# A transformer block with cross-attention on one core: the sums of proj_w are made beside the second group's attention instead of the first's

## The chip, the cores and the metric

The kernel runs on one core of a Trainium2 chip. The metric is the time in device microseconds (us) of one execution, and before stands at a median of 676.46 us. A core has a matrix engine, TensorE (PE; its weight loads are shown as PEld), three engines for work on elements, VectorE (DVE), ScalarE (ACT) and GpSimd (POOL), and the queue SP (SyncE) from which all transfers of this kernel are issued. TensorE multiplies one stationary tile with one moving tile and adds into a bank of PSUM; the other engines move results into SBUF.

## The reference

Eight sequences of 256 tokens with 512 channels (x) attend to eight contexts of 256 tokens (ctx_2048). The inputs are float32, and so are all products.

```python
x = layer_norm(hidden_states, ln1_w, ln1_b)
q = (x @ q_w + q_b).reshape(B, LQ, H, HD).transpose(0, 2, 1, 3)
k = (encoder_hidden_states @ k_w + k_b).reshape(B, LK, H, HD).transpose(0, 2, 1, 3)
v = (encoder_hidden_states @ v_w + v_b).reshape(B, LK, H, HD).transpose(0, 2, 1, 3)
scores = jnp.einsum('bhqd,bhkd->bhqk', q, k) * scale
scores = jnp.where(mask, scores, mask_value)
attn = jax.nn.softmax(scores, axis=-1)
out = jnp.einsum('bhqk,bhkd->bhqd', attn, v)
out = out.transpose(0, 2, 1, 3).reshape(B, LQ, D)
hidden = out @ cproj_w + cproj_b + residual
y = layer_norm(hidden, ln2_w, ln2_b)
y = jax.nn.gelu(y @ fc_w + fc_b, approximate=True)
return hidden + (y @ proj_w + proj_b)
```

There are 16 heads of 32 channels. fc_w is 512 x 2048 and proj_w is 2048 x 512.

## The kernel before, in words

**Groups and stages.** The eight sequences are two groups of four (g is 0 or 1). Per group: layer norm, the products q, k and v, the attention, the output product o, a second layer norm (norm_y, turn_y), the first product of the MLP (fc, with fc_w), gelu, and the second one (pd, with proj_w). Stages of the two groups overlap: while TensorE makes group 0's attention it also makes group 1's k, v and q, and while it makes group 1's attention it also makes group 0's o and fc.

**Strassen products.** Each large product is made by Strassen's scheme in Winograd's form: seven products of half-size blocks (P1 to P7) in place of eight, which needs sums of blocks of both operands ahead of the products. `quad` (line 837) makes the seven products with their evictions (t1, t2, t3, c11, c12, c21, c22: VectorE or ScalarE copies or adds a bank of PSUM to SBUF). The two MLP products use two levels, 49 small products; `grown2` (line 1212) and `grown` (line 1146) walk the outer seven in the order 1, 6, 2, 5, 3, 7, 4. So fc016_P5 is group 0, half 1 of the hidden columns, outer product 6, inner product 5.

**Sums of the MLP weights.** `mlp_weight_sums` (line 1062) makes them for a weight's half s (0 or 1): four quarters are loaded, four outer sums of 1024 columns (pw0s1 to pw0s4 for half 0 of proj_w), then for each of the seven outer operands four inner sums of 256 columns (pw0i6_1 and so on). Every sum may run on VectorE or on GpSimd. The results are stored to DRAM (prd0_6_False for an outer sum, prd0_6_True for the inner ones) and are read back piece by piece when the product pd needs them (loads pl). For proj_w that is 32 loads of 128 KB, 8 outer and 56 inner sums, and 22 stores; `proj_sums` (line 1094) issues them. fc_w has the same with fw, fcd and fl, and has no part in the change.

**One unit of attention.** A unit is one group, one set of four heads and one sequence: unit 121 is group 1, the third set of heads (8 to 11), sequence 1. `scores` (line 991) issues for it: the score product s121 (TensorE); eight evictions ev121 (ScalarE); two row maxima mx121 (VectorE, transposing as they reduce), a transpose mt and a fold of them on VectorE with three copies mc on ScalarE between; a store md and a load mm that spread the maximum over all partitions; two subtractions less121 (VectorE, or GpSimd in two pieces of 512 columns); two exponentials exp121 (ScalarE). `attend` (line 1039) then issues the attention product av121 (TensorE), its inverse of the row sums r121 (three instructions on VectorE) and the scaling att121. A group has 16 units (`units_of`); the written streams put av three units behind s.

**The order.** Nothing is decided at run time. The text `PROGRAM` (lines 124 to 353) names all 2927 steps in one fixed order, and a letter after a colon says which engine does a step that has a choice: V is VectorE, A is ScalarE, G is GpSimd; without a letter it is the step's first alternative. `Order.run` (line 94) goes through the words and issues the steps in that order, so each engine and the queue SP work through their own steps strictly in it:

```python
for word in PROGRAM.split():
    name, _, e = word.partition(":")
    o = ops.pop(name)
    o.eng = letters[e] if e else o.alts[0][0]
```

The text `PLACES` (lines 355 to 468) gives each buffer its slot of SBUF or its bank of PSUM in the same way; a slot is used by many buffers one after the other, and a step waits until the slot's earlier buffer has been read for the last time. Step names in the profile are buffers' names: pr holds a unit's scores and exponentials, mx its maxima, mm the spread maximum, rc and r the inverse, pw0s and pw0i sums of proj_w, h the result of fc, z1t and z1i sums of it ahead of pd, ps_y the transposes after the second layer norm.

**Where the sums of proj_w stand in before.** Between s000 and s100, the first score products of the two groups, the text has 60 of the 64 sums (24 on VectorE, 36 on GpSimd), 31 of the 32 loads and 19 of the 22 stores; the rest follow later. The lines of `PROGRAM` with s003 to av003 are 186 to 196, those with s121 to av121 are 232 to 244.

Of the kernel before, what the change touches and what calls it, by code (L numbers as in the profile page):

```python
# [148 lines left out]
ct1_3 mx000_1 fw1i7_1:G q0_0_P4 fw0i4_3:G q0_1_P7 q0_0_c21 aggr_x1_10 q0_1_c11 k0_0_c21 q0_1_P5 aggr_x1_11
fw0i3_2:V mt000 fw0i3_4:V mc000_2 fw1i6_1:V mc000_3 fcd0_3_True mc000_1 fw1i3_2:V s020 q0_1_t3:A fw1i6_2:V fold000  # L150
fw1i3_4:G q0_1_c22 q0_0_P3 md000 fw1i6_3:G ev020_01 ev020_30 fcd1_3_True eps_x1_1 ev020_10 pow_x1_1 ct1_7 ev020_31
ev020_21 fw1i7_2:G q0_1_P4 ev020_20 q0_0_c12:V fw0i4_1:G ev020_00 mx020_1 ev020_11 fw1i7_4:G s002 fw1i6_4:V
fcd1_7_True q0_1_c21 ct1_6 v0_0_P7 mx020_0 ct1_5 ev002_30 ev002_11 ct1_2 ev002_31 nb_x1_1 mt020 mm000 ev002_00
fw0i4_2:V ev002_10 fcd1_6_True v0_1_P7 mc020_3 v0_0_c22 mc020_2 pw0_00_01 ev002_01 fw0i4_4:V ev002_21 mx002_0
mc020_1 ev002_20 s022 mx002_1 q0_1_P3 ev022_20 fold020 ev022_10 ev022_31 mt002 v0_1_c22 md020 ev022_30 less000_0:G
ev022_21 vd0_0_12 turn_c1_31 ev022_11 kd0_0_22 turn_c1_21 ev022_01 mc002_1 turn_c1_00 kd0_1_11 ev022_00 v0_0_P4
# [199 lines left out]
cq0_00=42 cq0_10=82 cq0_01=60 cq0_11=58 ps_cols=3 ps_c0_00=0 c0_00=64 ps_c0_10=4 ps_c0_20=4 c0_10=46 ps_c0_30=3  # L356
ps_c0_01=0 c0_01=62 ps_c0_11=4 ps_c0_21=1 c0_11=56 ps_c0_31=4 xt0_0=34 xt0_1=58 xt0_2=32 xt0_3=63 xt0_4=83 xt0_5=33
xt0_6=14 xt0_7=23 st_x0_0=9 mv_x0_0=8 rs_x0_0=2 xn_x0_00=65 xn_x0_01=22 st_x0_1=4 mv_x0_1=5 rs_x0_1=4 xn_x0_10=5
# [1111 lines left out]
```

## Time and profile before

| | us |
|---|---|
| three runs | 677.11, 676.02, 676.46 |
| median | 676.46 |
| the profiled execution, its own time | 676.35 |
| its span, first to last instruction | 674.6 |
| TensorE busy | 663.8 (4001 matmuls) |
| VectorE busy | 578.3 (969 instructions) |
| GpSimd busy | 379.1 (340 instructions) |
| ScalarE busy | 340.1 (699 instructions) |
| mean granted clock of TensorE | 0.997 of full speed |

A row of the profile that groups instructions names the code line, the engine, the operation, the output and the inputs by their buffers with partitions x elements, the count after x, then the busy time in us and the mean duration of one in ns, then the idle time of the engine just before them and what ended most of it. A row with a time in front is one instruction, or several that run back to back: start, duration, engine, line, and in square brackets how long the engine had been idle and for whom. A row of TensorE's waits gives the total in us, the count and the longest. All matmuls have one line (641), so they are told apart by the buffer names. Times in these rows are us from the start of the span.

### The profile page before, as it was taken

Reading aid. Unit: us, or ns where it says so; the run is one execution under the profiler, and the core shown is the slowest. Engines: PE = TensorE matmul, PEld = TensorE weight load, DVE = VectorE, ACT = ScalarE, POOL = GpSimd, SP = SyncE. Lnnn points to the kernel's source line nnn. Section 1 sums busy time; section 2 is a strip of 40 time slices with the busy share of each in tenths; the row PEclk is TensorE's granted clock in tenths of the full one; section 3 lists DMA queues with packets and bytes.
Section 4 is the critical chain, followed back from the end, with each engine's and each line's share of the span. In section 5 each row is a group of like instructions: output and inputs, shape, how many; then the busy total and the mean of one; then the engine's idle time right before and its main releaser. Section 6 shows DMA issues by size and latency. Waiting matters only on the chain.

```text
span 674.6 us, 11523 instructions
## 1 busy us (share of the span) xinstructions
PE 663.8 (98%) x4001; PEld 498.3 (74%) x4001; DVE 578.3 (86%) x969; ACT 340.1 (50%) x699; POOL 379.1 (56%) x340
## 2 busy tenths in 40 slices
PE   9999999999899999999999999999999999999997
PEld 7674564478544676777687888888888888888886
DVE  2889889999999999999889999998489877896874
ACT  1246488768999979976764872001040221930000
POOL 1552556575578999977945743310636247518542
PEclk9999999999989999999999999999999999999999
DMA  8989888987957635445552646997999586842686
GB/s 264 329 273 337 306 286 257 295 258 211 307 164 241 210 113 203 157 142 170 174 190 95 220 130 167 267 245 250 165 243 237 133 243 149 232 144 57 192 166 118
DMA packets 173034, 140.65 MB, mean 209 GB/s; under 512 B 83712, under 2 KB 133424, under 8 KB 172976
## 3 DMA queue, kind: packets, MB, share of 16 engines
q1 hardware_dynamic: 172976, 139.92, 70.5%
q8 instruction: 32, 0.52, 0.3%
q14 instruction: 26, 0.21, 0.1%
HBM read 102.00 MB, written 37.88 MB: 207 GB/s over the span
## 4 chain that ended last, share of the span: by engine, by line
PE 92%; DVE 4%; DMA 3%; ACT 1%; issue 0%; SPq 0%; POOL 0%; DVEq 0%
PE fc_X L641 14%; PE pd_X L641 14%; PE fc_W L641 7%; PE pd_W L641 7%; PE av L641 6%; PE s L641 4%; PE k_X L641 4%; PE v_X L641 4%; PE q_X L641 4%; PE o_X L641 4%; PE pd_Y L641 4%; PE fc_Y L641 3%; PE k_W L641 2%; PE v_W L641 2%; PE o_W L641 2%; PE q_W L641 2%
## 5 line engine op out<-in xcount | busy, mean ns | idle before, releaser
L621 ACT ACTIVATE pr<-s,cols 128x256 f32<-128x256 f32 x256 | 103.1, 480 | 30.5 <-PE s L641 24.5
L1029 POOL TENSOR_TENSOR pr<-pr,mm 128x512 f32<-128x512 f32 x74 | 98.1, 1353 | 28.8 <-ACT pr L621 9.5
L1004 DVE TRANSPOSE_TENSOR_REDUCE mx<-pr 128x32 f32<-128x1024 f32 x64 | 77.6, 1222 | 1.9 <-ACT pr L621 1.8
L1209 ACT ACTIVATE h<-h,cols 128x256 f32<-128x256 f32 x128 | 54.6, 496 | 48.4 <-DVE h L632 45.5
L1032 ACT ACTIVATE pr<-pr 128x1024 f32<-128x1024 f32 x64 | 66.9, 1066 | 3.8 <-POOL pr L1029 2.9
L632 DVE TENSOR_TENSOR h<-fc_X,h 128x512 f32<-128x512 f32 x80 | 53.0, 678 | 10.0 <-PE fc_X L641 8.3
L641 PE MATMUL av<-pr,ones 128*32 128x256 f32 x512 | 35.1, 392 | 3.5 <-ACT pr L621 3.3
L632 DVE TENSOR_TENSOR h<-fc_W,h 128x512 f32<-128x512 f32 x48 | 32.1, 680 | 5.1 <-PE fc_W L641 4.9
L1024 DVE TENSOR_TENSOR pr<-pr,mm 128x1024 f32<-128x1024 f32 x27 | 34.8, 1310 | 0.9 <-DMA mm<-md 0.9
L1011 ACT COPY mx<-mx 32x64 f32<-32x64 f32 x96 | 23.3, 243 | 16.6 <-DVE mx L1008 13.4
L630 POOL TENSOR_TENSOR z1i<-z1t,z1i 128x512 f32<-128x512 f32 x12 | 16.8, 1420 | 26.0 <-issue 16.3
L641 PEld LDWEIGHTS av<-pr,ones 128*32 128x32 f32 x512 | 14.4, 110 | 21.8 <-issue 5.9
L632 POOL TENSOR_TENSOR h<-h,fl 128x512 f32<-128x512 f32 x16 | 21.4, 1350 | 8.6 <-DVE h L632 7.5
L613 ACT ACTIVATE e<-pd_X,cols 128x256 f32<-128x256 f32 x4 | 1.9, 468 | 44.1 <-PE pd_X L641 31.9
L641 PE MATMUL fc_W<-y1i,fl 128*128 128x256 f32 x92 | 22.8, 379 | 0.0
L641 PE MATMUL pd_X<-z1i,pl 128*128 128x256 f32 x96 | 22.0, 379 | 0.0
L796 POOL TENSOR_TENSOR rs_y<-rs_y,neg_half 128x2 f32<-128x2 f32 x8 | 8.2, 1034 | 23.4 <-DVE rs_y L793 22.8
L1012 DVE TENSOR_REDUCE mx<-mx 32x32 f32<-32x256 f32 x32 | 18.5, 580 | 2.4 <-ACT mx L1011 2.2
L641 PE MATMUL pd_W<-z1i,pl 128*128 128x256 f32 x88 | 20.5, 379 | 0.0
L641 PEld LDWEIGHTS pd_X<-z1i,pl 128*128 128x128 f32 x96 | 18.2, 190 | 2.5
L641 PEld LDWEIGHTS fc_W<-y1i,fl 128*128 128x128 f32 x92 | 17.5, 190 | 2.4
L641 PE MATMUL pd_X<-z0i,pl 128*128 128x256 f32 x80 | 19.0, 380 | 0.0
(593 smaller groups left out, 1836.3 us busy)
## 6 DMA issues: line engine op xcount, KB each, us to landing
mm<-md SPq DMA_DIRECT2D x32, 512.0 KB, 4.9
pl<-prd SPq DMA_DIRECT2D x52, 256.0 KB, 4.4
fl<-fcd SPq DMA_DIRECT2D x41, 256.0 KB, 4.1
fl<-prd SPq DMA_DIRECT2D x18, 256.0 KB, 4.6
fw<-in_L_xattn_fc_w_dram SPq DMA_DIRECT2D x16, 256.0 KB, 5.3
pw<-in_L_xattn_proj_w_dram SPq DMA_DIRECT2D x32, 128.0 KB, 3.1
hid<-in_x_dram SPq DMA_DIRECT2D x8, 512.0 KB, 3.6
hd<-hid SPq DMA_DIRECT2D x8, 512.0 KB
```

Of the source, the lines that this page charges most:

```text
L621: lambda e: nc.scalar.activation(to(), of_(), AF.Identity, bias=bias(), scale=1.0))
L630: nc.gpsimd.tensor_tensor(to()[:, ts(k, 512)], in0()[:, ts(k, 512)], in1()[:, ts(k, 512)], op)
L632: E[e].tensor_tensor(to(), in0(), in1(), op)
L641: nc.tensor.matmul(o(), l(), r(), start=first, stop=True, skip_group_check=True)
L796: lambda e, rs=rs: nc.gpsimd.tensor_tensor(tile_of(rs)[:, 2:4], tile_of(rs)[:, 0:2], neg_half[:, 0:2], ALU.pow), lock=True)
L1004: T.op(f"mx{u}_{h}", [("DVE", 1.126)], [(pr[h], None)], [(mx, [h])], lambda e, h=h: nc.vector.tensor_reduce(tile_of(mx)[:, 0:64].rearrange ...
L1011: lambda e, a=a: nc.scalar.copy(tile_of(mx)[0:32, 64 + 64 * a : 128 + 64 * a], tile_of(mx)[32 * a : 32 * a + 32, 64:128]))
L1012: T.op(f"fold{u}", [("DVE", 0.38)], [(mx, [2, 3, 4, 5])], [(mx, [6])], lambda e: nc.vector.tensor_reduce(tile_of(mx)[0:32, 320:352], tile_ ...
L1024: nc.vector.tensor_tensor(p_, p_, m_[:, :, None, :].to_broadcast([P, 2, 2, S]), ALU.subtract)
L1029: E[e].tensor_tensor(p_, p_, at(M, j)[:, None, :].to_broadcast([P, 2, S]), ALU.subtract)
L1032: lambda e, h=h: nc.scalar.activation(tile_of(pr[h]), tile_of(pr[h]), AF.Exp), table="exp")
L1209: lambda e, f=f, b=b, c=c: nc.scalar.activation(at(h[f][b], c), at(h[f][b], c), AF.Gelu_apprx_tanh, bias=col(c_fcb + f * 4 + c), scale=1.0 ...
```

## The change

The changed kernel differs only in the two texts `PROGRAM` and `PLACES`. It has the same 2927 steps, so the same products, sums, loads and stores, in another order, and 234 of them stand on another engine: VectorE gets 981 instructions in place of 969, ScalarE six fewer, GpSimd 11 fewer. The queue SP has the same 565 transfers in another order. 1040 of 1301 buffers have another slot.

The sums of proj_w move. In the first group's attention (s000 to s100) one sum and four loads are left. Three sums, ten loads and one store stand between s100 and the first transpose of the second layer norm (turn_y0_00). Between that and the last attention product (av133) stand 55 sums, 18 on VectorE (12 inner, 6 outer) and 37 on GpSimd, with 18 loads and 19 stores; five sums and two stores follow later. In the same stretch VectorE makes 8 halves of the subtractions less and GpSimd 11, where before it was 3 and 17.

All other steps keep their dependencies, but their order was written anew along the whole program, so the neighbours of nearly every step differ. Of the text the two stretches are shown that hold s003 to av003 and s121 to av121, before (-) and after (+), and the first line of the places.

```diff
 PROGRAM = """
...
-prd0_4_True v1_1_P3 less032_0:V norm_x1_20:A fold021 s003 v1_0_c22 md021 av001 pw1i4_4:V ev003_30 v1_0_c12:V
-pw1i1_3:G ev003_10 ev003_01 pw1i1_1:V ev003_31 pw1i1_2:V ev003_21 v1_1_P7 pw1i1_4:G ev003_11 pw1_01_10 exp032_1
-pw1s1:V pw1_01_00 pw1_01_01 ev003_20 ev003_00 pw1_01_11 r001 turn_x1_31 pw1s2:G exp032_0 prd1_4_True turn_x1_21
-turn_x1_11 mm021 mx003_1 x1_31:A av032 prd1_1_True v1_1_c12:A mx003_0 x1_21:A pw1i2_3:G mt003 q1_0_P1 pw1i2_1:G
-att001 mc003_3 v1_1_c22 x1_11:A pw1i2_2:G r032 mc003_2 mc003_1 pw1i2_4:G ab0_000 s023 fold003 pw1s3:V md003 v1_1_P4
-ev023_20 ku033 ev023_31 pw1i6_3:V ev023_21 prd1_7_False less021_0:V ev023_11 ev023_10 turn_x1_01 ev023_30 pw1i6_1:V
-v1_0_P4 ev023_00 mm003 less021_1:V ev023_01 prd1_6_False x1_01:A ow10 att032 exp021_1 pw1s4:G s011 vd0_1_21
-v1_0_c21 ku013 mx023_1 exp021_0 vd0_1_12 q1_1_P1 prd1_5_False ev011_30 mx023_0 ev011_00 pw1i6_2:G ev011_20 ev011_11
-av021 mt023 ev011_21 pw1i6_4:V ev011_10 x1t1:V prd1_6_True ev011_01 fl012_2 ev011_31 q1_0_t1:A less003_0:V s031
-mc023_1 mc023_2 mc023_3 pw1i7_1:V less003_1:V ev031_01 exp003_0 fold023 pw1i7_2:G exp003_1 mx011_0 md023 pw1i5_1:G
-ev031_21 vu013 x1t2:G ev031_20 r021 ev031_30 prd1_2_True av003 ev031_10 ev031_00 att021 ev031_31 mx011_1 ev031_11
...
+x1_20:V md001 v1_0_P5 x1_30:A less032_0:V x1_00:A nb_x1_2 v1_0_c11 s003 mm001 pw0_00_10 mt021 v1_0_t3:V v1_1_P2
+norm_x1_21:V ev003_30 mc021_2 norm_x1_31:V ev003_10 norm_x1_20:V mc021_1 ev003_31 v1_1_t3:V mc021_3 v1_0_P7
+ev003_11 fold021 ev003_20 v1_1_c11 ev003_01 md021 ev003_00 less001_0:V exp032_0 turn_x1_31 turn_x1_21 turn_x1_01
+x1_31:V x1_21:A turn_x1_11 x1_01:V ev003_21 v1_1_P3 mm021 x1_11:A less001_1:V pw0_00_01 exp001_0 v1_0_P3 x1t3:G
+v1_0_c22 exp001_1 mx003_0 s023 v1_0_c12:V mx003_1 v1_0_P4 ev023_21 ev023_30 mt003 ev023_31 less021_0:V ev023_11
+ev023_10 v1_1_P7 ev023_00 less021_1:V mc003_1 mc003_2 ev023_20 mc003_3 v1_0_c21 ev023_01 av001 exp021_0 v1_1_c22
+fold003 v1_1_c12:A mx023_0 md003 exp021_1 s011 vd0_1_22 x1t1:G r001 ow10 v1_1_P4 ev011_10 mm003 mx023_1 ev011_20
+ev011_11 ev011_01 ev011_31 x1t2:G mt023 att001 q1_0_P1 ev011_21 ev011_30 ev011_00 mx011_1 mc023_3 mc023_1 mc023_2
+s031 ab0_000 fold023 x1t4:G mx011_0 md023 av032 ev031_20 ow11 ev031_00 v1_1_c21 ev031_10 ev031_21 mt011 ev031_11
+mm023 av021 less003_1:G ev031_30 r032 vu033 ev031_01 ev031_31 pw0_00_11 mc011_3 att032 mc011_2 q1_0_t1:V pw0_00_00
+mc011_1 s013 mx031_1 less003_0:G exp003_1 q1_1_P1 mx031_0 fold011 q1_0_P6 less023_1:G q1_1_t1:V exp003_0 md011 r021
+ev013_21 ev013_01 q1_1_P6 mt031 ev013_10 att021 mm011 ev013_30 ows1:V ev013_11 mc031_1 less023_0:G q1_0_t2:V
+ev013_00 av003 ev013_31 mx013_0 ev013_20 mc031_3 mc031_2 exp023_1 fold031 s033 mx013_1 md031 ab0_100 hid0_0 q1_0_P2
...
-y0_21:A mt101 s121 fc001_t2:V fc011_t2:A mc101_2 r112 fc011_P5 less132_1:G ev121_01 fl016_2 ev121_31 fc001_c11
-mc101_3 fc001_P5 ev121_10 fc011_t3:V ev121_00 fc011_P7 mc101_1 att112 ev121_30 fold101 less132_0:G ev121_21
-fc011_P3 ev121_11 fc011_c22 md101 ev121_20 fl012_0 mx121_0 exp132_1 fc011_P2 s103 fc001_t3:A fc011_c12:V mm101
-y0i2_1:G fc011_c11 fc011_P4 ev103_30 mx121_1 exp132_0 fc001_P7 fl006_3 y0i2_2:V ev103_20 mt121 fl006_2 av132
-fc011_c21 ev103_11 ev103_10 fc001_c22 ev103_01 ev103_31 mc121_2 ev103_21 fc001_P4 mc121_3 r132 y0t2:G ev103_00
-mc121_1 fc001_P3 fold121 att132 s123 md121 fc001_c21 fl002_2 fc001_c12:V less101_0:G fc006_P1 ev123_21 ev123_10
-mm121 ev123_01 y0i6_1:V fc006_P2 fl012_3 mx103_1 ev123_11 ev123_31 fc016_P1 ev123_20 ev123_30 fc006_t1 y0i6_2:G
-exp101_0 fc016_P2 fc016_t1 less101_1:G fc006_P6 fc006_c11 fc016_c11 fc016_P6 fc006_t2 fc012_P1 mx103_0 y0i6_3:G
-exp101_1 fc006_P5 y0i2_4:G mt103 fc016_t2 mc103_1 y0i6_4:G mc103_3 av101 mx123_1 ev123_00 mc103_2 y0i2_3:G
-less121_1:G fold103 fc006_t3 s111 md103 mx123_0 fc006_P3 ev111_01 fl002_3 fc012_t1 ev111_00 less121_0:G mm103
-fc016_P5 mt123 r101 fl013_3 mc123_1 ev111_10 fc012_P2 mc123_2 fc006_c12 fc012_P6 fc012_c11 ev111_20 fc002_P1
-mc123_3 fc012_t2 exp121_1 fold123 fc012_P5 att101 ev111_11 md123 fc002_t1 ev111_21 fc006_P7 less103_1:G fl016_3
-exp121_0 mx111_0 fl006_1 fc002_P2 ev111_31 fl005_0 ev111_30 fc006_c22 av121 fc016_t3 less103_0:G mx111_1 fc002_P6
...
+fc011_t3:A pw0s1:V prd0_7_False y0_11:A fc011_P3 y0_01:A pw0s2:V prd0_5_False fc001_P5 exp132_0 fl001_1 s121
+pw0i6_1:V fc011_c12:A pw0i7_1:V pw0i6_2:V fc001_t3:A y0t1:V av132 ev121_20 mm101 ev121_21 ev121_11 fc001_c22
+pw0i6_4:G ev121_31 ev121_01 pw0i7_2:V fc001_P3 ev121_10 fl016_0 r132 pw0i7_3:G ev121_30 ev121_00 pw0i7_4:G mx121_1
+s103 pw0s4:G prd0_7_True prd0_6_False mx121_0 fc011_P7 ev103_10 fl012_0 ev103_20 ev103_30 fc001_P4 fc011_c22
+ev103_21 pw0i6_3:G ev103_11 mt121 fc011_P4 att132 ev103_00 less101_1:V ev103_31 mc121_2 ev103_01 fl006_1 mc121_1
+less101_0:V s123 prd0_6_True mc121_3 exp101_1 fold121 exp101_0 y0t2:G mx103_0 md121 ev123_01 fl012_3 av101
+fc001_c12:A fc001_c21 fl002_0 ev123_31 mx103_1 ev123_11 ev123_10 pw0i5_1:G ev123_20 fc006_P2 mt103 pw0i5_3:G mm121
+fc011_c21 mc103_3 ev123_00 pw1_10_10 fc006_P1 r101 pw0i5_2:G mc103_2 mc103_1 fl002_2 ev123_21 y0i6_1:G fc016_P1
+ev123_30 fc006_t1 pw0i5_4:G fold103 fc012_P1 y0i6_2:G fc006_c11 md103 fc012_P2 fc016_t1 y0i2_1:G prd0_3_False
+att101 fl002_3 pw0i3_3:G fc016_P2 fc012_t1 fl016_3 y0i2_2:G fc012_c11 fc016_P6 fl012_1 pw0i3_1:G mx123_1 s111
+pw0i3_2:G fc016_t2 less121_1:G fc006_P6 ev111_00 mx123_0 mm103 ev111_11 prd0_5_True ev111_01 fc012_P6 fc006_t2
+fc002_P1 less121_0:V exp121_1 fc006_P5 ev111_10 fc002_t1 pw0i3_4:G fc016_P5 exp121_0 mt123 y0i2_3:G fc016_c11
+fc002_P6 mc123_2 fl006_3 mx111_0 y0i6_4:G mc123_3 mc123_1 fl002_1 av121 y0i2_4:G fold123 less103_0:G fc012_t2 md123
...
 """

 PLACES = """
-cq0_00=42 cq0_10=82 cq0_01=60 cq0_11=58 ps_cols=3 ps_c0_00=0 c0_00=64 ps_c0_10=4 ps_c0_20=4 c0_10=46 ps_c0_30=3
...
+cq0_00=54 cq0_10=56 cq0_01=68 cq0_11=16 ps_cols=4 ps_c0_00=0 c0_00=80 ps_c0_10=4 ps_c0_20=2 c0_10=66 ps_c0_30=0
...
 """
```

628 lines of the change are left out of this document (313 added, 315 removed).

## The prediction

> **What bounds the kernel now.** I read the page first, then the busy time by stretches of the run, then what TensorE waited for, then the one stall by time. The page:
>
> ```profile
> span 674.6 us, 11523 instructions
> PE 663.8 (98%) x4001; PEld 498.3 (74%) x4001; DVE 578.3 (86%) x969; ACT 340.1 (50%) x699; POOL 379.1 (56%) x340
> ```
>
> TensorE is busy for 98% of the span, and the change alters no product: it can only add or remove waits of TensorE. VectorE is second with 86%, a mean over very unequal stretches (columns: busy time and instructions of TensorE, weight loads, VectorE, ScalarE, GpSimd, then granted clock, DMA share, GB/s):
>
> ```profile
> 59.50:162.40 102.90, 102.69 (x661) 60.53 (x660) 95.06 (x164) 72.98 (x157) 56.26 (x56) 1.00 0.86 279
> 162.40:186.90 24.50, 21.24 (x209) 13.10 (x208) 24.17 (x38) 22.45 (x48) 14.28 (x14) 0.99 0.79 257
> 186.90:190.30 3.40, 3.39 (x36) 1.47 (x36) 3.17 (x7) 2.39 (x8) 2.56 (x3) 0.56 0.61 205
> 190.30:270.00 79.70, 79.01 (x688) 48.74 (x688) 77.10 (x130) 73.31 (x158) 71.71 (x55) 1.00 0.57 183
> 270.00:381.70 111.70, 110.36 (x800) 84.45 (x796) 103.32 (x180) 80.64 (x153) 82.31 (x76) 1.00 0.51 164
> 495.00:674.60 179.60, 175.55 (x810) 152.04 (x809) 138.55 (x218) 38.27 (x86) 88.49 (x76) 1.00 0.68 172
> ```
>
> The first score product (s000) starts at 59.5, the first transpose of the second normalization (turn_y0_00) at 270.0, the last attention product (av133) at 381.7. From 162.4 to 270 VectorE has almost no idle time: 24.17 of 24.50 us, then 77.10 of 79.70. From 270 on it is at 92% (103.32 of 111.70). TensorE loses its time in one place:
>
> ```profile
> PE av L641 <- ACT pr L621: 3.3, 1, 3.3
> PE ps_y L728 <- DVE att L632: 1.1, 1, 1.1
> PE ps_c L728 <- DMA cq<-in_ctx_dram: 0.3, 1, 0.3
> ```
>
> ```profile
> 183.82 1.22 DVE L1024 TENSOR_TENSOR pr<-pr,mm 128x1024 f32<-128x1024 f32 x1
> 184.09 2.04 ACT L1032 ACTIVATE pr<-pr 128x1024 f32<-128x1024 f32 x2
> 186.91 1.93 PE L641 MATMUL av<-pr,ones 128*32 128x256 f32 x16 [3.27 <-ACT pr L621]
> 188.62 1.67 PE L641 MATMUL av<-pr,xt 128*32 128x256 f32 x16
> ```
>
> At 183.6 TensorE has nothing left but the attention product of unit 003 (av003). Its exponentials run from 184.09, because VectorE's subtraction (less003) came only at 183.82. From s003 to av003, 162.4 to 186.9, VectorE worked through 38 instructions without a break, ten of them sums of proj_w. The idle 3.27 us have a second price: the clock was 0.56 in the next 3.4 us, and av003 took 186.91 to 190.22, 3.3 us.
>
> **The change, part by part.** Times are against the profiled execution, 676.35 us (span 674.6 and 1.75 around it), 0.1 below the median 676.46. Under 0.2% (1.35 us) I count as the same. The durations that I use:
>
> ```profile
> L1004 DVE TRANSPOSE_TENSOR_REDUCE mx<-pr 128x32 f32<-128x1024 f32 x64 | 77.6, 1222 | 1.9 <-ACT pr L621 1.8
> L632 DVE TENSOR_TENSOR h<-fc_X,h 128x512 f32<-128x512 f32 x80 | 53.0, 678 | 10.0 <-PE fc_X L641 8.3 <-POOL h L632 1.2 <-DMA mm<-md 0.2
> L1024 DVE TENSOR_TENSOR pr<-pr,mm 128x1024 f32<-128x1024 f32 x27 | 34.8, 1310 | 0.9 <-DMA mm<-md 0.9
> L1012 DVE TENSOR_REDUCE mx<-mx 32x32 f32<-32x256 f32 x32 | 18.5, 580 | 2.4 <-ACT mx L1011 2.2
> L1058 DVE STREAM_TRANSPOSE r<-rc 128x256 f32<-128x256 f32 x32 | 14.3, 446 | 1.1
> L1055 DVE TRANSPOSE_TENSOR_REDUCE rc<-av 128x8 f32<-128x256 f32 x32 | 13.6, 424 | 1.3 <-PE av L641 1.3
> L632 DVE TENSOR_TENSOR att<-av,r 128x256 f32<-128x256 f32 x32 | 12.8, 408 | 0.5
> L1008 DVE STREAM_TRANSPOSE mx<-mx 128x64 f32<-128x64 f32 x32 | 7.5, 234 | 0.6
> L1057 DVE RECIPROCAL rc<-rc 128x8 f32<-128x8 f32 x32 | 6.5, 203 | 1.1
> L632 DVE TENSOR_TENSOR x1t<-x,x 128x1024 f32<-128x1024 f32 x1 | 1.2, 1215 | 0.0
> L632 DVE TENSOR_TENSOR pw0i<-pw0s 128x256 f32<-128x256 f32 x4 | 1.6, 407 | 0.0
> L1029 POOL TENSOR_TENSOR pr<-pr,mm 128x512 f32<-128x512 f32 x74 | 98.1, 1353 | 28.8 <-ACT pr L621 9.5 <-DVE mx L1012 6.0 <-DMA mm<-md 3.6
> L632 POOL TENSOR_TENSOR pw0i<-pw0s 128x256 f32<-128x256 f32 x4 | 2.8, 724 | 0.0
> 162.43 1.08 PE s L641 x16
> 163.51 1.86 PE av L641 x32
> 158.98 3.45 PE v_X L641 x16
> 548.83 5.26 PE fc_X L641 x24
> ```
>
> Check of the method on the old stall. The 38 instructions are 5 maxima (mx), 4 subtractions, 3 inverses of three instructions each (0.446 + 0.424 + 0.203 = 1.07), 2 scalings, 2 folds, 2 transposes, 7 inner and 2 outer sums of proj_w, one x1t, 4 evictions: 6.1 + 5.2 + 3.2 + 0.8 + 1.2 + 0.5 + 2.8 + 3.6 + 2.7 = 26.2 us of durations, measured as 24.17 us busy, since neighbours overlap; factor 0.92. TensorE's work there is 4 scores, 3 attention products, 3 v and 2 q products (q at about v's 1.73), 4 transposes: 4.3 + 5.6 + 5.2 + 3.5 + 1.8 = 20.4 us. Deficit 3.8, idle time measured 3.27. So this count gives a stall some 0.5 us too large.
>
> Removed: proj_w's sums from the first group's attention. Between s000 and s100 before issues 24 of the 64 sum steps on VectorE and 36 on GpSimd, 31 of 32 loads and 19 of 22 stores; after keeps one sum and four loads there. From s003 to av003 TensorE now has 5 scores, 7 v, 4 q and 3 attention products and 4 transposes, 5.4 + 12.1 + 7.1 + 5.6 + 1.8 = 32.0 us. VectorE has 17 steps of 512 columns, 8 mx, 4 subtractions, 4 folds, 3 inverses, 3 scalings, 5 transposes: 11.5 + 9.8 + 5.2 + 2.3 + 3.2 + 1.2 + 1.2 = 34.4, times 0.92 = 31.6. So the stall of 3.27 goes (minus 3.3), and with it the slow clock: av003 falls from 3.3 to 1.86 (minus 1.4). Nothing else in 59.5 to 162.4 can be won: TensorE was busy 102.69 of 102.90.
>
> Added: the same sums between turn_y0_00 and av133. There now stand 18 sum steps on VectorE (12 inner, 6 outer), 37 on GpSimd, 18 loads and 19 stores. Five more subtractions come to VectorE too (8 in place of 3), since GpSimd is taken. The tight place is unit 121. From s121 to av121 TensorE has 4 scores, 2 attention products and 17 first-MLP products: 4.3 + 3.7 + 17 x 0.877 = 22.9 us (before had 25 such products there). VectorE has 41 instructions: 7 mx, 13 evictions, 3 subtractions, 2 inverses, 2 scalings, 2 folds, 3 transposes, 4 inner sums, one y0t: 8.6 + 8.8 + 3.9 + 2.1 + 0.8 + 1.2 + 0.7 + 1.6 + 1.2 = 28.9, times 0.92 = 26.7 us. Deficit 3.8, less the 0.5 of the check: plus 3.3. A wider count agrees: in the whole stretch VectorE gets 12 x 0.407 + 6 x 1.215 + 5 x 1.31 + 4 x 0.678 + 1.2 of new work and loses some 4.4 (two inverses and their followers), net 18.3, times 0.92 = 16.8 us, onto 103.3; TensorE's work there grows by ten products, 8.7 us, onto 111.7. That is 120.1 of 120.4 us. VectorE's best share so far over a long stretch is 77.10 of 79.70 (96.7%); at that share 120.1 us need 124.2, plus 3.8. Bounds: 0 (units before the place give enough lead) and 3.8 with a slow clock, 5.2. I take 3.3, the count at the unit itself.
>
> The clock behind the new stall. Before, an idle 3.27 us was followed by 3.4 us at 0.56, while the 1.1 us before ps_y left the clock at 1.00 (190 to 381.7). In the new place the products in between are themselves fed by evictions on VectorE, so the lack should come in bits of about a microsecond: 0, bounds 0 and 1.4. [...]
>
> The wait before ps_y (1.1). From o0_1_P4 to turn_y0_00 VectorE has 33 instructions in place of 34, and TensorE one score more (1.08), which gives lead; but the two normalizations that feed the transpose last move from VectorE to ScalarE. Between 0 and minus 1.1; I take minus 0.6.
>
> Loads, stores, queues. The 28 later loads (128 KB) and the stores stand on SP between the row-maximum transfers (md, mm) of the second group; a store waits for its sum and holds what is behind it. GpSimd gets 35 inner sums (0.724) and two outer (2 x 1.35), and loses six subtractions (2 x 1.35 each): 25.3 + 5.4 - 16.2 = 14.5 us onto 82.3, 97 of 120 us, less than the 71.71 of 79.70 it bore before 270. The DMA share was 0.86 in the first group and 0.51 in the second, where the transfers go: 0. The first use of a proj_w sum as operand lies some 50 us of TensorE work behind its store. The opening order differs, but TensorE waited for loads only 0.3 us there, and the bytes ahead of each early product are about the same: 0, bounds minus 0.3 and plus 1. At the end four transposes follow the last product, in place of two: plus 0.2, at most 0.6.
>
> Sum: 676.35 - 3.3 - 1.4 + 3.3 - 0.6 + 0.2 = 674.55, say **674.6 us**, 0.3% under the median. Its own range, from the bounds of the three small terms, is 673.5 to 676.5.
>
> **The rivals.**
> 1. The new stall is one gap. The 1.4 of the slow clock come back: 676.0, no change. For it: av121 waits for an exponential as av003 did. Against: 17 short products with evictions stand before it.
> 2. VectorE bounds the whole second attention (slower). 120.1 of 120.4 us leaves no time to catch up. If each instruction there takes 3% more than my prices, through more GpSimd work beside it, 123.7 us at a share of 96.7% need 127.9: plus 7.5 in place of 3.3, 678.8, and 680.2 with a slow clock. It decides from 1.2% on, where 121.5 / 0.967 is 125.7 and the gain of 5.3 is used up. For it: a 128x1024 sum took 1215 ns above, and takes 1565 here:
>
> ```profile
> L632 DVE TENSOR_TENSOR z1i<-z1t,z1t 128x1024 f32<-128x1024 f32 x7 | 10.9, 1565 | 0.8 <-PE pd_X L641 0.8
> ```
>
> Against: from 190 to 270 VectorE ran at 97% beside a GpSimd busy for 71.71 of 79.70 us, and TensorE idled 0.7 us.
> 3. The new sums are hidden. GpSimd takes one half of unit 121's subtraction, and later units have their scores ahead; the plus 3.3 falls away: 671.2. For it: the 77.10 of 79.70 before 270 cost TensorE almost nothing. Against: the old stall followed the count of VectorE to half a microsecond.
> That the sums stay where they were is excluded: the order of the instructions is fixed in the program.
>
> **How the numbers follow.** Forecast 0.38, rival 1 0.10, rival 2 0.36, rival 3 0.16. I place the forecast's own spread as 0.29 below 675.1 and 0.09 within 1.35 us of the median; with rival 3 faster has 0.45, the same 0.19 with rival 1, slower 0.36. For 8 in 10 the range leaves out the ends of rivals 2 and 3: 671.2 to 680.5.
>
> **What would show it.** Right: no wait of 3.3 us for an exponential before 270 and no clock under 1.00 at 183 to 190; VectorE at 99% from turn_y0_00 to av133; waits of TensorE for VectorE or ScalarE of 2 to 4 us in sum between 270 and 345, near s121 to av121, at clock 1.00. Wrong: TensorE waits of more than 5 us there, or a new wait for prd, pl or mm; a stall left in the first group; losses after 495, where VectorE takes over GpSimd's sums of z1.

## The result, and the profile after

In 22 runs of each kernel on the same chips the changed kernel took 677.56 us (675.83 to 679.68), the kernel before 676.43: a ratio, formed chip by chip, of 1.0023, 95% interval 1.0016 to 1.0031. It is slower by 0.23% where 0.3% faster was forecast (674.6); the range of 671.2 to 680.5 holds it. The profiled execution took 679.25 us, 1.7 above its median, while that of before lay at its median. So the 2.9 us between the two spans overstate the 1.1 us between the medians.

The page of the changed kernel, first rows:

```profile
span 677.5 us, 11498 instructions
PE 666.5 (98%) x4001; PEld 498.2 (74%) x4001; DVE 589.9 (87%) x981; ACT 334.8 (49%) x691; POOL 347.6 (51%) x329
```

TensorE's waits, and the busy time by stretches (columns as before):

```profile
PE av L641 <- ACT pr L1032: 1.9, 2, 1.4
...
PE fc_W L641 <- POOL h L632: 0.8, 1, 0.8
```

```profile
155.60:199.80 44.20, 43.05 (x359) 26.34 (x358) 43.18 (x66) 37.56 (x84) 25.52 (x20) 1.00 0.41 131
...
282.00:308.50 26.50, 25.07 (x201) 17.82 (x202) 26.09 (x42) 18.86 (x45) 22.52 (x25) 1.00 0.90 280
...
345.00:391.00 46.00, 45.11 (x252) 36.54 (x250) 43.30 (x69) 25.18 (x40) 36.70 (x37) 1.00 0.77 242
```

The wait of 3.3 us is gone, as forecast; so is the slow clock behind it. From s121 (282.1) to av121 (308.5) VectorE is busy for 26.09 of 26.50 us, as counted. Yet no wait exceeds 1.4 us there. And TensorE idles 0.9 of the 46.0 us from 345 to 391, where the forecast had nothing; the kernel before had lost none of its time there:

```profile
345.00:381.70 36.70, 36.70 (x217) 30.31 (x215) 34.20 (x54) 22.53 (x36) 24.65 (x21) 1.00 0.47 152
```

The waits do not add up to the loss, since many are shorter than those rows show. So for every kernel I took the starts of all TensorE steps in order and subtracted each step's undisturbed duration, read from the profiles (score 1.08, av 1.75, v, o and pd 1.73, k and q 1.72, fc 0.86, transpose 0.44). The remainder is lost time. The columns are stretches between equal amounts of TensorE work done (641.9 us in all), so kernels with another order can be compared. "End" runs from the start of the last step to the end of the span. Each row is one profiled execution; rows of kernels whose text is the same up to 160 differ by up to 1.4 us there, so only repeated differences count. All in us:

| kernel | span | 0-160 | 160-200 | 200-260 | 260-280 | 280-340 | 340-400 | 400-642 | end |
|---|---|---|---|---|---|---|---|---|---|
| before | 674.6 | 10.4 | 6.5 | 5.0 | 1.0 | 3.2 | 0.3 | 2.0 | 4.2 |
| after | 677.5 | 10.7 | 3.1 | 4.1 | 3.6 | 3.5 | 2.6 | 3.1 | 4.8 |
| before_nosum | 675.2 | 11.0 | 6.3 | 5.5 | 1.0 | 3.0 | 0.3 | 2.0 | 4.2 |
| before_exp003 | 672.5 | 9.4 | 6.2 | 4.6 | 1.0 | 3.0 | 0.3 | 2.0 | 4.1 |
| before_acts | 673.8 | 10.7 | 6.3 | 4.5 | 1.0 | 3.0 | 0.3 | 2.0 | 4.1 |
| before_best | 674.8 | 10.8 | 6.7 | 4.9 | 1.0 | 3.0 | 0.3 | 2.0 | 4.2 |
| after_nosum | 673.9 | 9.7 | 1.9 | 3.8 | 3.6 | 3.2 | 2.4 | 3.1 | 4.3 |
| after_fc007 | 674.6 | 9.8 | 3.1 | 3.6 | 3.6 | 3.6 | 1.2 | 3.1 | 4.7 |
| after_tail | 676.3 | 9.8 | 1.9 | 3.6 | 3.6 | 3.5 | 2.7 | 4.7 | 4.6 |
| after_two | 674.3 | 9.7 | 1.9 | 3.6 | 5.3 | 3.3 | 1.2 | 3.1 | 4.3 |
| after_three | 673.1 | 9.8 | 1.9 | 3.6 | 3.7 | 3.6 | 1.2 | 3.1 | 4.3 |

After less before: -3.4 (the old stall) and -0.9 (the wait before ps_y) against +2.6 (near unit 101), +2.3 (fc003 to fc014), +1.1 and +0.6 (what follows 400, and the end), and small terms of +0.6: 2.9.

### The profile page after: what moved, and what is told of

It is laid out like the page before. It is cut to its first block, busy times and chain, and to the rows that moved or that the text cites. A ratio compares the mean times of both kernels' runs of the same rounds, so it can differ in the third digit from the quotient of the medians.

```text
span 677.5 us, 11498 instructions
## 1 busy us (share of the span) xinstructions
PE 666.5 (98%) x4001; PEld 498.2 (74%) x4001; DVE 589.9 (87%) x981; ACT 334.8 (49%) x691; POOL 347.6 (51%) x329
## 4 chain that ended last, share of the span: by engine, by line
PE 73%; DVE 13%; ACT 5%; issue 3%; DMA 3%; POOL 2%; SPq 0%; DVEq 0%; POOLq 0%; ACTq 0%
PE pd_X L641 14%; PE fc_X L641 12%; PE pd_W L641 7%; PE fc_W L641 6%; DVE mx L1004 4%; PE av L641 4%; PE k_X L641 4%; PE pd_Y L641 4%; PE fc_Y L641 4%; PE v_X L641 3%; ACT pr L621 2%; PE s L641 2%; PE o_X L641 2%; PE k_W L641 2%; DVE h L632 2%
## 5 line engine op out<-in xcount | busy, mean ns | idle before, releaser
L621 ACT ACTIVATE pr<-s,cols 128x256 f32<-128x256 f32 x256 | 103.9, 482 | 28.2 <-PE s L641 19.6
L1029 POOL TENSOR_TENSOR pr<-pr,mm 128x512 f32<-128x512 f32 x80 | 100.5, 1284 | 8.3 <-DMA mm<-md 8.2
L1032 ACT ACTIVATE pr<-pr 128x1024 f32<-128x1024 f32 x64 | 66.5, 1061 | 8.7 <-POOL pr L1029 5.3
L630 POOL TENSOR_TENSOR z1i<-z1t,z1t 128x512 f32<-128x512 f32 x2 | 2.5, 1268 | 55.8 <-DVE z1t L632 55.8
L1024 DVE TENSOR_TENSOR pr<-pr,mm 128x1024 f32<-128x1024 f32 x24 | 29.6, 1253 | 0.5 <-DMA mm<-md 0.5
L807 ACT ACTIVATE xn_y<-hid,rs_y 128x512 f32<-128x512 f32 x12 | 9.4, 812 | 37.6 <-DVE rs_y L799 32.4
L641 PE MATMUL pd_W<-z1i,pl 128*128 128x256 f32 x104 | 24.4, 379 | 0.0
L641 PE MATMUL pd_X<-z0i,pl 128*128 128x256 f32 x96 | 22.5, 380 | 0.0
L641 PEld LDWEIGHTS pd_W<-z1i,pl 128*128 128x128 f32 x104 | 19.8, 190 | 2.7
L641 PE MATMUL pd_W<-z0i,pl 128*128 128x256 f32 x88 | 20.7, 380 | 0.2 <-issue 0.2
L641 PEld LDWEIGHTS pd_X<-z0i,pl 128*128 128x128 f32 x96 | 18.2, 190 | 2.9 <-DVE po L853 0.4
L632 POOL TENSOR_TENSOR po<-po,e 128x256 f32<-128x256 f32 x12 | 10.3, 874 | 18.4 <-DVE e L632 11.6
```

The source lines that it names most:

```text
L621: lambda e: nc.scalar.activation(to(), of_(), AF.Identity, bias=bias(), scale=1.0))
L630: nc.gpsimd.tensor_tensor(to()[:, ts(k, 512)], in0()[:, ts(k, 512)], in1()[:, ts(k, 512)], op)
L632: E[e].tensor_tensor(to(), in0(), in1(), op)
L641: nc.tensor.matmul(o(), l(), r(), start=first, stop=True, skip_group_check=True)
L807: nc.scalar.activation(tile_of(xn), f(), AF.Identity, bias=tile_of(rs)[:, 4 + i : 5 + i], scale=tile_of(rs)[:, 2 + i : 3 + i])
L1024: nc.vector.tensor_tensor(p_, p_, m_[:, :, None, :].to_broadcast([P, 2, 2, S]), ALU.subtract)
```

## The experiments

A letter behind a step's name is its engine, as in `PROGRAM`. Each time is a median, with the ratio to runs of the kernel before on the same chip. The intervals are about 0.1% wide to either side, so effects under a microsecond are read from the profiles.

**Without the sums.** Both kernels, with the 64 sums left out and their transfers kept.

```diff
-            plus(f"{name}{i}", d, a[0], b[0], dv, a[1], b[1], n, op=op, pool_too=pool_too)
+            if not name.startswith("pw"):
+                plus(f"{name}{i}", d, a[0], b[0], dv, a[1], b[1], n, op=op, pool_too=pool_too)
...
-                  lambda: tile_of(b).rearrange("p (e m) -> p e m", e=4), 0.52)
+                  lambda: cb.t[:, None, :256].to_broadcast([P, 4, 256]), 0.52)
```

> The kernel before without the 64 sums of proj_w, in the same way. If the old stall at 183.6 is made by the ten sums between s003 and av003, as the prediction counted, the idle 3.27 us and the slow clock behind it (1.4 us) go: 676.4 - 4.7 = 671.7 us, and TensorE's granted clock is 1.00 from 183 to 190. If the stall has another cause, it stays and the time is 676 us.

> The changed kernel without the 64 sums of proj_w (the loads and the stores stay, the stores write 256 columns of a bias row in place of the sums, so the last product gets a wrong weight). Theory A, the price of the sums in their new place is a VectorE that cannot keep up: the wait of av101 for its exponentials (1.43 us in the profile of the changed kernel) and the small losses around it, 2.6 us between the first fc products and s111, go, and the wait before fc013_P4 (0.82 us) goes too, as VectorE has 18 instructions fewer there: 677.6 - 2.6 - 0.9 = 674.1 us. Theory B, the sums are hidden in their new place and the rest of the new order is what costs (a VectorE sum ows1 of 3.19 us at 187.3, four transposes after the last product): within 0.7 us of 677.6, and the two places still show their waits.

Before without sums: 676.52 (1.0006, 0.9994 to 1.0019), no change. After without sums: 676.80 (1.0013, 1.0001 to 1.0025). TensorE's waits of the one, then of the other (line numbers shifted by the edit):

```profile
PE av L635 <- ACT pr L615: 3.2, 1, 3.2
PE ps_y L722 <- DVE att L626: 1.1, 1, 1.1
```

```profile
PE av L636 <- ACT pr L1028: 1.4, 1, 1.4
...
PE fc_W L636 <- POOL h L627: 0.5, 1, 0.5
```

Every wait that was to be VectorE's is still there, nearly to the tenth: 3.2 for 3.3, 1.4 for 1.4. Theory A in the expectations, that VectorE's load makes the waits, was the ground of the forecast; it falls at both places. The sums cost nothing that can be measured in their old place. In their new place the two ratios differ by 0.001, some 0.7 us, and the intervals overlap. The whole stretch from turn_y0_00 to av133 says the same, with the sums and without them:

```profile
267.00:391.00 124.00, 121.27 (x840) 91.97 (x836) 118.89 (x195) 84.57 (x162) 99.22 (x102) 1.00 0.79 250
```

```profile
264.50:387.40 122.90, 120.59 (x844) 92.25 (x841) 106.22 (x177) 84.97 (x163) 65.01 (x61) 1.00 0.79 250
```

VectorE has 12.7 us less to do there, and TensorE needs only 1.1 us less.

**The old stall.** The subtractions of unit 003 first, nothing else:

```diff
-mt023 ev011_21 pw1i6_4:V ev011_10 x1t1:V ... less003_0:V s031 ... pw1i7_1:V less003_1:V
+mt023 ev011_21 less003_0:V less003_1:V pw1i6_4:V ev011_10 x1t1:V ... s031 ... pw1i7_1:V
```

> The kernel before with one edit: the two subtractions of unit 003 stand ahead of a sum of proj_w, a sum of x1t and another sum of proj_w on VectorE, 2.0 us of work, with nothing taken away. If VectorE's order is what makes the stall, av003 starts some 2.1 us earlier, the gap of 1.2 us that is left keeps the clock at 1.00 (as 1.1 us before ps_y did), and the time is 676.4 - 2.1 - 1.4 = 672.9 us. If the maximum of unit 003 lands too late for an earlier subtraction, nothing moves and the time is 676.4. If a gap of 1 us is enough for the slow clock, 674.3.

676.12 (0.9998, 0.9989 to 1.0007). The timeline around the stall, one row for each run of like instructions:

```profile
180.07 2.32 DVE L1024 TENSOR_TENSOR pr<-pr,mm 128x1024 f32<-128x1024 f32 x2
...
181.65 1.15 PE L641 MATMUL s<-k,ku 32*128 32x256 f32 x16
...
182.87 0.47 ACT L621 ACTIVATE pr<-s,cols 128x256 f32<-128x256 f32 x1
...
183.24 1.99 ACT L1032 ACTIVATE pr<-pr 128x1024 f32<-128x1024 f32 x2
...
185.13 2.65 ACT L621 ACTIVATE pr<-s,cols 128x256 f32<-128x256 f32 x7
...
186.01 1.93 PE L641 MATMUL av<-pr,ones 128*32 128x256 f32 x16 [3.22 <-ACT pr L621]
```

The subtractions end at 182.39, well ahead of the exponentials' turn at 183.24, and av003 waits as long. The bracket says why, and said so before: L621 is the eviction of scores, not the exponential (L1032). `PLACES` gives av003 bank C3, which held the third part of s031's scores. ScalarE evicts in order: one eviction, two exponentials, then two evictions, of which the second frees C3. The wait is a loop from TensorE to TensorE (s031, ScalarE's queue, the bank, av003). No head start of TensorE's inputs shortens it. So the order on ScalarE was changed next (less003 stays early, as in the run before):

```diff
-ev011_31 q1_0_t1:A ... s031 mc023_1 mc023_2 mc023_3 ... ev031_01 exp003_0 ... exp003_1 ... ev031_21 ... ev031_20 ... ev031_30 ... av003
+ev011_31 exp003_0 s031 exp003_1 ev031_21 ev031_20 q1_0_t1:A mc023_1 mc023_2 mc023_3 ev031_01 ev031_30 av003
```

> The kernel before with the order on ScalarE and VectorE changed around the old stall, nothing taken away: the subtractions of unit 003 and then its two exponentials stand ahead of the copies and evictions that separated s031 from av003, and the two evictions that free the PSUM bank which av003 writes (s031's third) come right behind them. Theory C, a loop through ScalarE and a bank (s031, its evictions, the exponentials between them, av003): av003 can start 2.8 us after the start of s031 in place of 4.4, the gap falls from 3.2 to some 1.6 us, and the time to 676.3 - 1.6 = 674.7 us, or 673.3 if the slow clock behind the gap goes too. Theory A, VectorE sets the gap: VectorE has the same work, the gap stays at 3.2 us and the time at 676.3.

675.81 (0.9994, 0.9984 to 1.0004).

```profile
PE av L641 <- ACT pr L621: 1.5, 1, 1.5
PE s L641 <- ACT pr L621: 1.4, 1, 1.4
```

```profile
184.50:188.00 3.50, 2.13 (x38) 1.26 (x33) 3.16 (x7) 3.14 (x10) 3.50 (x4) 1.00 0.51 149
```

The wait before av003 fell to the 1.5 us that the loop gives, and the clock stayed at 1.00. But s013 now waits 1.4 us for the evictions that were put off: 6.2 us lost in the stretch against 6.5. The next two runs go after that.

> As the kernel before with the exponentials of unit 003 early, and now all eight evictions of s031 stand on ScalarE ahead of the three copies of unit 023 and the eviction q1_0_t1, which had pushed them back: in the run before it, TensorE idled 1.47 us before av003 and then 1.37 us before s013, which needs the banks of those evictions. Theory C (ScalarE's order sets when s013 gets its banks): 1.4 us less work of ScalarE stands ahead of s013, so its wait falls to some 0.2 us: 675.8 - 1.2 = 674.6 us, under both kernels. If the copies, now late, hold unit 023 in its place, the gain comes back as a wait of av023: 675.8.

All eight evictions ahead of the copies (on VectorE r021 and att021 also pass fold023): 675.64 (0.9988, 0.9978 to 0.9999), the one kernel whose interval lies wholly under the kernel before; among so many runs, one that close to 1 may be chance. The loss moved on, with 6.3 us in the stretch:

```profile
188.12 1.13 PE L641 MATMUL s<-xt,ku 32*128 32x256 f32 x12 [0.18 <-DVE att L632]
...
191.90 1.98 PE L641 MATMUL q_X<-x1t,kws 128*128 128x512 f32 x4 [0.73 <-ACT vw L613]
```

The first row is s013. Its other 4 matmuls ran from 187.24; these 12 wait for att021 on VectorE, the last reader of bank C0, which holds s013's third part. So q1_0_P6 behind s013 comes 0.86 us late through VectorE, not through an eviction of q. The second row is q1_1_P6, which does wait for an eviction of q that ScalarE now does late. The next run moves both evictions to VectorE (q1_0_t1, q1_1_t1 from `:A` to `:V`, and earlier in the text):

> The kernel before with the exponentials of unit 003 and the evictions of s031 early, as in the run before it, and two evictions of the product q (q1_0_t1, q1_1_t1; 0.7 us each) moved from ScalarE to VectorE, which is the fuller engine there. Theory C (ScalarE's order holds TensorE): the waits before q1_0_P6 and q1_1_P6 in the run before (0.86 and 0.99 us longer than a product) go, 675.6 - 1.6 = 674.0 us. Theory A (VectorE): VectorE gets 1.4 us more where it has no idle time, so the time rises to 677.

675.95 (1.0002, 0.9992 to 1.0013). Now s013 waits longer for VectorE:

```profile
PE av L641 <- ACT pr L621: 1.5, 1, 1.5
...
PE q_X L641 <- ACT k L613: 0.9, 1, 0.9
...
PE s L641 <- DVE att L632: 0.8, 1, 0.8
```

ScalarE's order made the wait of 3.2 us; once that is shortened, VectorE and ScalarE hold TensorE by turns, and VectorE has no room to take ScalarE's work. Each edit moved the loss within 160 to 200 and took at most 0.3 us out of it.

**The wait before av101.** Two evictions from ScalarE to VectorE ahead of s121's, with the sums and without them:

```diff
-pw0i6_1:V fc011_c12:A pw0i7_1:V pw0i6_2:V fc001_t3:A y0t1:V av132
+pw0i6_1:V fc011_c12:V pw0i7_1:V pw0i6_2:V fc001_t3:V y0t1:V av132
```

> The changed kernel with two evictions of the first fc product (fc011_c12, fc001_t3; 1.1 us on ScalarE) moved from ScalarE to VectorE, just ahead of the evictions of s121. They tell the two theories of the wait before av101 (1.43 us) apart. Theory A, VectorE bounds here: it gets 1.36 us more, the wait grows to some 2.8 us, 678.9 us. Theory C, the chain goes through ScalarE (evictions of s121, s103 and s123 with the exponentials between them): the wait shrinks by 0.3 to 1.1 us, to 0.3 to 1.1, 676.9 us. If it is the load of the maximum, whose slot of SBUF is given free by s121, the wait stays at 1.43, 677.6.

> The changed kernel without the 64 sums of proj_w (as before: stores write a bias row), and with the two evictions fc011_c12 and fc001_t3 on VectorE, which now has room. If the wait before av101 (1.43 us with the sums and without them) goes through ScalarE's queue, it shrinks by 0.3 to 1.1 us. If it goes through the load of the maximum, whose slot s121 frees, it stays at 1.4.

With the sums 679.85 (1.0050, 1.0035 to 1.0066); without them 676.70 (1.0013, 0.9997 to 1.0028) and the wait unchanged at 1.4. The waits with the sums:

```profile
PE fc_W L641 <- DVE h L632: 1.6, 1, 1.6
PE av L641 <- ACT pr L1032: 1.6, 1, 1.6
```

So with the sums VectorE has no room here: 1.36 us more on it made a second wait of 1.6 us. Taking 18 sums away does not shorten the wait before av101, though. Nor does taking the two evictions from ScalarE, against what the theory of ScalarE's queue expected: they stand ahead of s121's evictions, and behind those ScalarE idles 1.22 us anyway, until s103 gives it work. In nosum_act101:

```profile
285.95 2.66 ACT L616 ACTIVATE pr<-s,cols 128x256 f32<-128x256 f32 x7 [1.22 <-PE s L636]
```

The chain of the changed kernel that ended last, cut to this place:

```profile
286.20 1.44 PE s L641 x16
...
288.00 2.29 ACT pr L621 x6
...
290.31 0.24 ACT mx L1011
...
290.57 0.47 ACT pr L621
...
291.07 0.24 ACT mx L1011
...
291.32 0.24 ACT mx L1011
...
291.59 0.67 ACT pr L1032
...
292.55 1.05 ACT pr L1032
...
293.64 0.40 PE av L641
```

From s103's evictions to av101 everything in this chain is ScalarE, in its written order: evictions, three copies of unit 121, two exponentials. Two runs without the sums change that order:

> The changed kernel without the 64 sums, with the maximum of unit 101 in another slot of SBUF, so that its load need not wait for s121, its subtractions ahead of the maxima of unit 121 on VectorE and its exponentials ahead of three copies on ScalarE. If the loop from s121 over the slot, the load, the subtraction and the exponential sets av101, its wait falls from 1.43 to some 0.4 us; unit 121, whose maxima come 2.4 us later, may get a wait of up to 1.5 us in turn. If something else sets it, the wait stays at 1.4.

> The changed kernel without the 64 sums, and with the two exponentials of unit 101 ahead of two of the three copies of unit 121 on ScalarE; nothing else is moved. Theory C (the chain from s103 through ScalarE's queue): the first exponential starts 0.5 us earlier, when its subtraction is just done, and the second waits for its own subtraction, so the wait before av101 falls from 1.43 to some 1.0 us. If the load of the maximum sets it, the subtractions come no earlier and the second exponential only follows them: the same 1.0 or more. If neither, 1.43.

nosum_slot: 676.37 (1.0004, 0.9994 to 1.0015), wait 0.76 us. nosum_mc, which moves only the exponentials past two copies: 676.46 (1.0009, 0.9998 to 1.0020), wait 1.03 as forecast.

```profile
289.14 1.07 PE L636 MATMUL av<-pr,ones 128*32 128x256 f32 x16 [0.76 <-ACT pr L1028]
```

```profile
291.56 1.07 PE L636 MATMUL av<-pr,ones 128*32 128x256 f32 x16 [1.03 <-ACT pr L1028]
```

So the order on ScalarE sets 0.4 us of this wait. What is left of it goes through VectorE's order, as nosum_mc shows:

```profile
288.08 2.34 DVE L1020 TENSOR_TENSOR pr<-pr,mm 128x1024 f32<-128x1024 f32 x2
...
289.32 2.19 ACT L1028 ACTIVATE pr<-pr 128x1024 f32<-128x1024 f32 x2
```

The second exponential begins when the second subtraction of unit 101 has ended, at 290.4, and the subtractions stand behind the maxima of unit 121. nosum_slot puts them ahead of those, and the wait fell further, to 0.76. So the written order of both engines makes the wait, with the sums and without them. Whether the slot that s121 frees has a part in it stays open, as nosum_slot moved the load, the subtractions and the exponentials at once. Neither gained time: nosum_mc lost some 3.6 us in the stretch as before, and in nosum_slot the product behind av101 waited 1.3 us for a sum on GpSimd.

**The losses that the forecast had not.** One sum of fc from VectorE to GpSimd (`fc007_11:V` to `:G`):

> The changed kernel with one sum of 512 columns (fc007_11) on GpSimd in place of VectorE, where it took 1.80 us beside a sum on GpSimd. If that sum is what holds the eviction which fc013_P4 waits for, the wait of 0.8 to 1.0 us at 377 goes: 676.7 us. If another instruction of GpSimd or ScalarE holds it, as the profile's releaser (GpSimd) says, the wait stays, and the time is 677.6 or, with GpSimd later by 1.3 us, up to 678.4.

676.29 (0.9996, 0.9983 to 1.0010): level with the kernel before, and 2.6 us lost between 340 and 400 became 1.2. Of these 1.4 the wait before fc013_P4 is 0.9 (it came 0.98 us late, and now 0.13); the rest is in part spread, since profiles without this edit lost 1.6 to 2.7 us here. In the changed kernel:

```profile
374.06 1.80 DVE L632 TENSOR_TENSOR h<-h,vws 128x512 f32<-128x512 f32 x1
...
377.58 0.68 DVE L632 TENSOR_TENSOR h<-fc_W,h 128x512 f32<-128x512 f32 x1
...
378.35 0.89 PE L641 MATMUL fc_W<-y0i,fl 128*128 128x256 f32 x3 [0.82 <-POOL h L632]
```

The sum took 1.80 us, and the eviction at 377.58, which fc013_P4 needs, came behind it on VectorE. The bracket names GpSimd; the edit shows that it was VectorE. Without the sums of proj_w this wait is still 0.5 of 0.8 us (the rows of after_nosum above), so they are not its main cause.

> The changed kernel with the sum ows1 (a sum of cproj_w) on GpSimd, in its idle time at 192.9, in place of VectorE beside a subtraction on GpSimd. Theory B1: its 3.19 us on VectorE (other sums of 512 columns take 0.69) are what makes TensorE idle before q1_1_P5 and lengthen q1_0_P5, 1.4 us in all: these go, 677.6 - 1.4 = 676.2 us. If the 2.5 us are only given back by the next wait: within 0.5 us of 677.6 and the idle time moves to av011 or av031.

ows1 (a sum of cproj_w) on GpSimd: 676.65 (1.0009, 1.0000 to 1.0017), and 2.0 us lost between 160 and 200 in place of 3.1. But after_tail, which does not have that edit, lost 1.9: the last section says why.

> The changed kernel with the end of the kernel before: its last product is pd14_P2 and two transposes follow it, in place of four after pd14_P4. If the longer end costs what the two profiles show (6.1 us from the end of the last product to the end of the span, against 4.9), 677.6 - 1.2 = 676.4 us. If the prediction's price holds (0.2, at most 0.6), 677.4 to 677.0.

The end of the kernel before in the changed one: 678.73 (1.0038, 1.0026 to 1.0051), slower. The end took 4.6 us in place of 4.8, but seven of the ten profiles with the changed kernel's own end have 4.3, so no gain is shown. And TensorE lost 1.6 us just before it, at pd14_P5, from whose place behind pd14_P6 the product pd14_P2 had been taken away:

```profile
PE pd_X L641 <- issue: 1.7, 1, 1.7
```

The 1.2 us that the two profiles seemed to show can't be had back by this order.

> The changed kernel with three of these edits together: ows1 on GpSimd, fc007_11 on GpSimd, the end of the kernel before. If the three losses are separate and nothing behind takes them back, 677.6 - 1.1 - 0.8 - 1.2 = 674.5 us, under the kernel before. If each is given back at the next wait, 677.

677.29 (1.0013, 1.0002 to 1.0024): the end's 1.6 us took back what the two sums gave. Without it:

> The changed kernel with ows1 and fc007_11 on GpSimd and its own end. fc007_11 alone gave 676.29, and ows1 alone 676.65, of 677.56. If the two are separate, 677.56 - 1.27 - 0.9 = 675.4 us, under the kernel before; if ows1's was chance (one kernel without that edit lost no time there either), 676.3.

675.55 (0.9992, 0.9980 to 1.0003), where the changed kernel had a ratio of 1.0023. With the exponentials of unit 101 ahead of two copies as well:

> The changed kernel with ows1 and fc007_11 on GpSimd and with the exponentials of unit 101 ahead of two copies on ScalarE. In the changed kernel the second subtraction ends at 292.2, so the second exponential can start 0.35 us earlier and no more: the wait before av101 falls from 1.43 to 1.1 us, and the time from 675.55 to some 675.2. If the later fold of unit 121 costs a wait before av121, 675.6 to 676.5.

675.64 (0.9994, 0.9983 to 1.0005): the wait fell to 1.0 us, near the 1.1 expected; the time did not fall.

## Why the prediction was wrong

**What was asked of the old stall: size right, cause wrong.** It went (160 to 200: -3.4 us, forecast -4.7 with the clock; -4.6 where ows1 was short). But the step "because VectorE's subtraction came only at 183.82" is false. The row that it rested on names ScalarE's evictions (L621); without any sum, and with the subtractions early, the stall stays at 3.2 us; with another order on ScalarE it falls to 1.5. The count of VectorE's work gave 3.8 us for 3.27 by coincidence (it has nine sums of proj_w, not the ten named above it). In the new order av003 again writes the bank of s031's third part (C0), but av032, av021, s013 and three products of q stand between them. That this is why the stall went is read from the texts; that the sums' move is not why follows from before_nosum.

**The slow clock, -1.4: right.** Behind a gap of 3.2 us it came in three profiles of three (granted clock 0.56, 0.53 and 0.62 in the 3.4 to 3.6 us behind it), and it was gone in the three where the gap fell to 1.5 us (1.00).

**The new stall, +3.3: nearly right in size, wrong in cause.** 2.6 us were lost, one unit earlier than forecast. VectorE's work was counted well: 118.9 us in a stretch of 124.0, forecast 120.1 in 124.2, and more work there costs time (after_act101). But the step that VectorE's count sets the deficit fails, and that the wider count fits is luck: with 12.7 us less on VectorE the stretch is still 122.9 us long, and the wait before av101 stays at 1.4. TensorE waits for a chain through both ScalarE's and VectorE's written order. The forecast did not count ScalarE at all, though the windows showed it at 22.45 of 24.50 us at the old stall.

**The wait before ps_y, -0.6:** the loss there went from 1.5 to 0.2 us: -1.3.

**The end, +0.2, at most 0.6:** +0.6 in this profile, and some 0.4 more among the last steps; but +0.1 in seven of the nine others with this end, so the term was about right.

**What the sum left out decided the sign.** The forecast compared the two stretches it had a reason to look at and set the rest to nothing. This is the step that failed in the number: the sum has one term for the whole second attention, taken at unit 121, and none for what lies between that unit and the end, without a reason. Between 340 and 400 the new order lost 2.3 us more. About 1 us of it is the wait behind one sum of fc put on VectorE at the wrong moment; moving that one step makes the kernel level with the one before. The rest, and 0.7 in pieces of 0.1 to 0.2 us behind 400, were not traced. With these and the end at its measured 1.0 the forecast's own terms give 674.6 + 2.3 + 0.7 + 0.8 = 678.4, on the measured side; the sizes are those of a profile that lay 1.7 us above its median of 677.6.

**The rivals.** "Sums hidden" was nearest in mechanism and furthest in time, because its 671.2 left the same terms out. "VectorE bounds the second attention" had the sign, and after_act101 shows its condition, no room on VectorE. But the sums are not what TensorE waits for there: without them the ratio is 1.0013 in place of 1.0023, and the intervals overlap.

## What to carry to other kernels

Read which instruction the bracket behind a wait names, by its line, before counting the engine that looks full; where it names an eviction, look up which bank or slot is being freed and follow the loop back to TensorE. Then test it with an edit: before fc013_P4 the bracket named GpSimd, and the edit showed VectorE. Here the wait inside such a loop moved to the next loop when it was shortened: 3.2 us before av003 became 1.5 there and 1.4 before s013 (before_exp003). When a whole schedule is replaced, price every stretch of it, not only the one that the change is about: here the forgotten stretches were worth more than the sums.

## What the runs showed of the hardware that was not expected

**The same sum on VectorE beside GpSimd took 0.7 us in five profiles and 3.2 in two.** It is ows1, first in the changed kernel, then in after_tail, with the piece of a subtraction that GpSimd began just behind it:

```profile
187.29 3.19 DVE L632 TENSOR_TENSOR q<-q,vws 128x512 f32<-128x512 f32 x1
...
187.43 1.27 POOL L1029 TENSOR_TENSOR pr<-pr,mm 128x512 f32<-128x512 f32 x1
```

```profile
186.34 0.71 DVE L632 TENSOR_TENSOR q<-q,vws 128x512 f32<-128x512 f32 x1
...
186.45 1.73 POOL L1029 TENSOR_TENSOR pr<-pr,mm 128x512 f32<-128x512 f32 x1
```

Of eight profiles with ows1 on VectorE, two had it at 3.2 us, five at 0.7 and one at 1.35. The two lost 1.2 us more between 160 and 200. In the other six GpSimd's piece took 1.7 us in place of 1.27. So between these rows one of the two took longer: ows1 by 2.5 us in the first pair (3.19 against 0.71), the piece by 0.46 in the second (1.73 against 1.27). The order in which they began does not tell them apart: in both profiles ows1 began 0.1 us ahead of GpSimd's piece, and in the first it still ended only after that piece and the next, at 190.48. The text up to there is the same in four of the eight kernels, one of them with 3.18 us and two with 0.71 beside the changed kernel's 3.19. So which of the two takes longer differs from run to run, and by my estimate, from the 1.2 us above, part of the spread of one kernel's times is of this kind. What makes the one or the other longer is not shown.

**Behind a gap of 1.4 to 1.6 us the clock was slow in two profiles of twelve.** The stretch behind av101 in the runs after_ows1 and after_two, and the same in the changed kernel, each behind a wait of 1.4 us:

```profile
291.80:295.20 3.40, 3.36 (x32) 1.38 (x32) 2.69 (x5) 3.34 (x10) 3.40 (x5) 0.51 0.96 253
```

```profile
290.90:294.30 3.40, 3.36 (x33) 1.66 (x34) 2.96 (x6) 3.34 (x10) 3.40 (x5) 0.61 0.94 242
```

```profile
293.60:297.00 3.40, 3.36 (x39) 2.27 (x40) 3.33 (x7) 3.34 (x10) 3.40 (x5) 1.00 1.02 242
```

Of twelve profiles with a gap of 1.4 to 1.6 us two were slow behind it (0.51 and 0.61; 1.00 in the other ten), and lost 1.7 us more (5.3 in place of 3.6 between 260 and 280). What sets these two apart is not shown. The prediction took a gap of about a microsecond to leave the clock at 1.00, as the 1.1 us before ps_y did; at 1.4 us the two profiles show 0.51 and 0.61.
